# Weighting the norm and the split in the co-run with an attention's convolutions

## Chip, cores and metric

The kernel runs on one NeuronCore of a Trainium2 chip. The metric is the device time of one execution in microseconds. Three runs of the kernel before took 6441.66, 6464.38 and 6468.22 us; their median is 6464.38 us.

## What is computed

Two layers work on four images x of 96 channels and 128 x 128 pixels, in float32. The first is a state-space block with four scans over the pixels; the second is an attention made of convolutions. Cut to what matters here:

```
# layer 0, its end: LayerNorm over the 192 channels of ym, a 1x1 projection, the residual
yn = (ym - mean(ym, channel)) * rsqrt(var(ym, channel) + 1e-5) * ln_w + ln_b
x  = x + einsum('bdhw,cd->bchw', yn, out_w) + out_b
# layer 1, on group-normalised x
xr, x1, x2 = relu_split_norm(gn(x))        # positive part, negative part, each normalised over the whole image
key   = unfold(conv3x3(x1, aw1)); qry = unfold(conv3x3(x2, aw2))
attn  = softmax(key . qry / sqrt(C*9))     # one 96 x 96 x 9 kernel per image
y1    = layer_norm(conv3x3(conv3x3(x1, aw3), attn))
y2    = layer_norm(conv3x3(x2, w_conv2)) * x1
x     = x + xr + conv1x1(concat(y1, y2), w_full) + b_full
...
```

## The kernel before

The work is cut into generators. Each emits a few instructions, yields a cost (a number that the author chose, roughly microseconds), and goes on when it is asked again. Two of them are interleaved by `co_run(left, right, pace)` (L298): after each step of `left`, what it cost times `pace` is added to a debt, and `right` is advanced until the costs that it yields have paid the debt. So a smaller cost on the right means more of its steps beside one step on the left. Nothing else decides how densely two pieces of work lie beside each other; the order in which the built program issues then follows the emission closely, with small moves. [...]

The pieces that matter:

- **The norm**, `ssm_output` (L931), called by `Image.norm`: the end of layer 0 for one image, in 16 tiles of 1024 pixels and two more rounds for the pipeline's ends. A tile goes through loading y on SP's queue (L946), squares on ACT (L950), sums on PE (L960), a copy st (L972 or L974), four small transfers mq from st on ACT's queue (L979), a variance on DVE (L986 to L988), a root on ACT (L992), a reciprocal (L996), a write of rd to DRAM (L998) and a read back spread over 96 partitions as r (L1006), both on POOL's queue, the projection on PE (L1012), the product with r on DVE (L1025 or L1027), the residual on POOL (L1033 or L1035), statistics on DVE (L1039) and the store of xnew on SP's queue (L1088). The steps of one tile are spread over three rounds of six steps. The costs of an image sum to 149.6.
- **The split**, `split_norm` (L1091), called by `Image.split`: a first pass over 16 tiles (ACT L1137 and L1144, DVE L1140; cost 2.4 a tile), and a second pass (ACT L1253, DVE L1257) which also makes six planes of each half, for the x1 half on ACT and POOL (L1418 to L1432), for the x2 half on DVE (L1396 to L1410), at 6 x 2.5 a tile. It has almost no work on PE. The costs of image 1, 2 or 3 sum to 278.4.
- **The close**, `attn_output` (L2289), called by `Image.close`: the last 1x1 convolution and the residuals, 16 tiles, four DVE passes (L2274, L2279, L2280, L2316) and two sums (L2327 or L2329) a tile; cost 83.2 (166.4 for image 2).
- **The attention**, `attention` (L1949): 11 strips of 12 rows. In the map stage each strip runs `products` (L1446) four times: matmuls at L1467 and L1482, then evacuation by ACT (L1540) and DVE (L1554 to L1562). The transposes and products of the attention kernel (L1760, L1635) go between. A softmax follows (`weights`, with the transposes at L1701 in it), and the value stage, 11 strips with the kernel just made. The costs of an image sum to some 503. The attention also issues the loads of strips that lie two ahead (`ya`, L1903, copied to `yb` by ACT at L1928), and where these need the next image's planes, `until` (L2473) would force the split on.
- **The direct maps** of image 0, `direct_maps` (L2116): the same maps as plain 3x3 convolutions (matmuls at L2159), evacuated by ACT (L2177).

The order at the end of the program is: norm and split of image 0 beside the scan (L2546, pace 0.65); the direct maps of image 0 beside the scan and, when that is done, beside `light`, which is norm 1 and split 1 (L2560, pace 1.0); then for each image b its attention on the left, and on the right what is left of `light` and, chained behind it, norm b+1, split b+1 and the close of image b-1 (L2588 to L2608). Before images 2 and 3 what is left of `light` is drained without anything on the left.

Of the kernel before, what the change touches and what calls it, by code (L numbers as in the profile page):

```python
# [71 lines left out]
def kernel(  # L72
# [225 lines left out]
    def co_run(left, right, pace):  # L298


        owed = 0.0
        for cost in left:
            owed += cost * pace
            while owed > 0:
                got = next(right, 0)
                if got == 0:
                    return
                if got is None:
                    owed = 0.0
                    break  # L310
                owed -= got
# [39 lines left out]
    def chain(*gens):  # L351
        for g in gens:
            yield from g

    def drain(gen):
        for _ in gen:
            pass
# [68 lines left out]
    def project(b, weights, mv, beside, zb, xrows, ps):  # L426
# [10 lines left out]
        with tc.tile_pool(name="a2", bufs=2, side="left") as p2:  # L437
            each = len(beside)
            beside = chain(*(run(p2, 2, queue) for run, queue in beside))
            later, parts = Later(), {}  # L440
            y0s = []
# [1994 lines left out]
    class Image:  # L2436
# [50 lines left out]
    zb, yms = (  # L2487
        [dram.tile(shape, F32, name=f"{n}{p}", tag=f"{n}{p}", bufs=1) for p in range(npair)]
        for n, shape in (("zb", [2, 2 * C, NU, H, UW]), ("yms", [2, 2 * C, L]))
    )  # L2490
# [21 lines left out]
    with tc.tile_pool(name="wp", bufs=1, side="left") as wp:  # L2512
# [30 lines left out]
    imgs = {0: Image(0)}  # L2543
    imgs[0].begin()
    left = chain(imgs[0].norm(yms[0][0], psl, "left"), imgs[0].split(psl, "left"))
    co_run(left, last, 0.65)  # L2546
    drain(left)
# [5 lines left out]
    psr = ctx.enter_context(tc.tile_pool(name="psr", bufs=2, space=PSUM, side="right"))  # L2553
    imgs[1] = Image(1)
    imgs[0].lifting = True
    light = chain(
        imgs[1].norm(yms[0][1], psr, "right"),
        imgs[1].split(psr, "right", lambda i, second: second),
    )
    co_run(left, light, 1.0)  # L2560
# [22 lines left out]
    def maps_made(last):  # L2583
        maps_only.close()
        pool = ctx.enter_context(tc.tile_pool(name="e2", bufs=1, side="left"))
        last.kept = pool.tile([C, NS, SN], F32, name="e2")

    for b in range(NB):  # L2588
        after = []
        if b:  # L2590
            if b > 1:
                drain(light)
            imgs[b].begin()
            if b + 1 < NB:
                imgs[b + 1] = Image(b + 1)
                after.append(imgs[b + 1].norm(yms[(b + 1) // 2][(b + 1) % 2], psr, "right"))
                after.append(
                    imgs[b + 1].split(psr, "right", lambda i, second: second)
                )
            after.append(imgs[b - 1].close(psr, "right", 1.0 if b + 1 < NB else 2.0))  # L2600
            if b + 1 == NB:
                last = imgs[b].last = LastOutput(imgs[b], psr, "right")
                imgs[b].maps_made = lambda: maps_made(last)
                after += [last.before(), last.beside()]
        light = chain(light, *after)
        left = imgs[b].attend(at)
        co_run(left, light, 1.0 if b else 1.5)
        drain(left)  # L2608
# [79 lines left out]
```

## Time and profile before

| what | value |
|---|---|
| median of three runs | 6464.38 us |
| the profiled execution: time, span | 6470.83 us, 6468.9 us |
| busy share of the span: PE, DVE, ACT, POOL | 82%, 73%, 59%, 50% |
| mean granted clock of PE | 0.889 |
| busy share of the 16 DMA engines | 65.2% on q1, 2.2% on q0, 0.9% on q10 |

In the lines of the profile PE is TensorE, PEld its weight loads, DVE VectorE, ACT ScalarE, POOL GpSimd and SP the engine that issues most transfers. L1467 is a line of the kernel, printed as it was before the change. `out<-in` are names of tiles. A busy share is an average over stages with different limits, so it is the table of stages that has to be read; the prediction shows it. An fp32 matmul appears as two instructions, a transpose as one. After the scan ends near 3240 us, the stages follow one another in the order told above: the attention of image 1 begins near 3822 us, that of image 2 near 4700 us, that of image 3 near 5700 us, and the last output near 6428 us.

### The profile page before, as it was taken

What the parts mean: (1) busy time and instruction counts of PE and PEld (TensorE: products, weight loads), DVE (VectorE), ACT (ScalarE), POOL (GpSimd) and SP (SyncE); (2) the same over time, 40 slices, a digit from 0 to 9 for tenths busy, and PEclk for the clock granted to TensorE, in tenths of its full rate; (3) what the DMA queues carried; (4) which work ended last, traced back from release to release, by engine and by line L of the source; (5) the groups of instructions that cost most, each with busy time, mean ns of one, the idle gap of its engine ahead of it and who ended that gap; (6) DMA issues with size and microseconds to landing.
All of it is one profiled execution on the core that took longest, in us unless ns stands there. A gap on an engine that the chain in (4) does not pass through costs nothing. (4 is left out here: it accounts for less than half of the span.)

```text
span 6468.9 us, 76257 instructions
## 1 busy us (share of the span) xinstructions
PE 5321.3 (82%) x23264; PEld 2301.3 (36%) x23264; DVE 4711.2 (73%) x7132; ACT 3786.8 (59%) x4770; POOL 3238.6 (50%) x2472
## 2 busy tenths in 40 slices
PE   6889988987888753989988588877888877989888
PEld 2333323322222111444433234345333445345553
DVE  4247778988989668988934785468874587888757
ACT  1247767776787676777632565466533665545642
POOL 1226757978889544979821344346213266022310
PEclk9999989998998665999999799888988988999989
DMA  6767777775675766675666776665766655966668
GB/s 154 176 157 193 191 202 196 218 213 163 199 198 163 214 173 215 197 217 174 199 182 185 187 220 161 164 157 155 213 195 164 178 145 155 243 174 181 191 170 219
DMA packets 891433, 1205.18 MB, mean 186 GB/s; under 512 B 228533, under 2 KB 743483, under 8 KB 878545
## 3 DMA queue, kind: packets, MB, share of 16 engines
q1 hardware_dynamic: 860496, 1145.35, 65.2%
q0 software_dynamic: 16208, 38.41, 2.2%
q10 hardware_dynamic: 14320, 16.54, 0.9%
q8 instruction: 187, 3.06, 0.2%
q14 instruction: 222, 1.81, 0.1%
HBM read 777.82 MB, written 345.62 MB: 174 GB/s over the span
## 5 line engine op out<-in xcount | busy, mean ns | idle before, releaser
L629 PE MATMUL bank<-y,wp 128*128 128x512 f32 (+3 forms) x3584 | 1320.2, 626 | 84.5 <-DMA y<-y 40.9
L862 POOL TENSOR_TENSOR y<-y,dl 128x1024 f32<-128x1024 f32 x384 | 1062.5, 2767 | 273.1 <-DVE dl L854 247.9
L829 POOL TENSOR_TENSOR dl<-dl,u 128x1024 f32<-128x1024 f32 x384 | 1015.8, 2645 | 247.1 <-ACT dA L805 129.5
L850 DVE TENSOR_TENSOR_SCAN dA<-dA,pBC 128x512 f32<-128x512 f32 x768 | 981.6, 1278 | 30.7
L1467 PE MATMUL two<-ya,wd 128*64 128x192 f32 (+3 forms) x2376 | 590.6, 422 | 201.7 <-ACT odd L1540 77.1
L629 PEld LDWEIGHTS bank<-y,wp 128*128 128x128 f32 (+3 forms) x3584 | 459.3, 169 | 755.8 <-issue 658.0
L854 DVE TENSOR_TENSOR dl<-dA,pBC 128x512 f32<-128x512 f32 x768 | 528.4, 688 | 260.0 <-PE pBC L743 187.1
L2159 PE MATMUL bank<-y,wn 128*64 128x384 f32 (+5 forms) x2408 | 665.2, 501 | 52.7 <-DMA y<-x1d 28.3
L743 PE MATMUL pBC<-xr,wbc 60*128 60x512 bf16 (+1 forms) x1536 | 458.5, 405 | 301.3 <-DVE dA L850 230.9
L1928 ACT COPY yb<-ya 64x768 f32<-64x768 f32 (+1 forms) x660 | 537.5, 814 | 202.6 <-PE two L1467 128.7
L672 ACT ACTIVATE dl<-pd,dtb 128x512 f32<-128x512 f32 x768 | 486.3, 684 | 183.2 <-PE pd L743 166.8
L1467 PE MATMUL two<-yb,wd 128*64 128x192 f32 (+3 forms) x2376 | 566.4, 407 | 4.0 <-ACT yb L1928 4.0
L833 DVE TENSOR_TENSOR pBC<-dl,pBC 128x512 f32<-128x512 f32 x768 | 527.5, 687 | 8.1 <-POOL dl L829 7.1
L2159 PEld LDWEIGHTS bank<-y,wn 128*64 128x64 f32 (+3 forms) x2408 | 306.9, 167 | 340.2 <-issue 150.9
L805 ACT ACTIVATE dA<-dl,negA 128x1024 f32<-128x1024 f32 x384 | 420.3, 1142 | 2.3
L1467 PEld LDWEIGHTS two<-ya,wd 128*64 128x64 f32 (+1 forms) x2376 | 266.9, 169 | 399.5 <-ACT odd L1540 87.8
L672 ACT ACT_TABLE_LOAD x248 | 318.2, 1283 | 94.9 <-PE pd L743 81.6
L743 PEld LDWEIGHTS <-wbc 60*128 60x128 bf16 (+1 forms) x1536 | 102.9, 96 | 749.3 <-issue 736.1
L1467 PEld LDWEIGHTS two<-yb,wd 128*64 128x64 f32 (+1 forms) x2376 | 295.1, 170 | 153.6 <-issue 41.5
L1012 PE MATMUL bank<-y,outws 96*96 96x512 f32 x512 | 313.6, 752 | 11.4 <-DVE r L1025 8.7
L1467 PE MATMUL two<-ya,wa 128*96 128x384 f32 (+1 forms) x528 | 229.9, 519 | 72.1 <-DMA ya<-vp 27.4
L1540 ACT COPY odd<-two 128x384 f32<-128x384 f32 (+5 forms) x176 | 116.0, 659 | 286.7 <-PE two L1482 177.2
(316 smaller groups left out, 9210.2 us busy)
## 6 DMA issues: line engine op xcount, KB each, us to landing
u<-zb SPq DMA_DIRECT2D x192, 1024.0 KB
yms<-y SPq DMA_DIRECT2D x96, 512.0 KB
y<-yms SPq DMA_DIRECT2D x64, 768.0 KB
xn<-xnew SPq DMA_DIRECT2D x128, 384.0 KB
ya<-vp SPq DMA_DIRECT2D x120, 336.0 KB
y<-y SPq DMA_DIRECT2D x128, 258.2 KB
zb<-z SPq DMA_DIRECT2D x64, 512.0 KB
ya<-x1p SPq DMA_DIRECT2D x90, 336.0 KB
```

The source lines that it names most:

```text
L629: nc.tensor.matmul(blocks(pz[p:e]), lhsT=ws[k][:, d, c : c + e - p], rhs=window(ys[k], at, d, n), start=(i == 0), stop=(i == len(terms) - 1),)
L672: nc.scalar.activation(dst, src, AF.Softplus, bias=bias)
L743: nc.tensor.matmul(p, lhsT=w[rows], rhs=xr[rows, at : at + CH], start=True, stop=True)
L805: nc.scalar.activation(live[m]["dA"], live[m]["dl"], AF.Exp, scale=negA[:, g % 3, k : k + 1])
L829: nc.gpsimd.tensor_mul(t, t, u_view(n))
L833: nc.vector.tensor_mul(p, live[n]["dl"][:, bass.ts(half, CH)], p)
L850: nc.vector.tensor_tensor_scan(h, h, p, init, ALU.mult, ALU.add)
L854: nc.vector.tensor_mul(live[n]["dl"][:, sl], live[n]["dA"][:, sl], live[n]["C", half])
L862: nc.gpsimd.tensor_add(v, v, t.rearrange("p (a b) -> p a b", b=W))
L1467: nc.tensor.matmul(of(to[p:e], r), lhsT=w[:, i, c : c + e - p], rhs=tiles(t[k][PAIR[i]][:, SLOT[i]], o, r), start=(k == 0), stop=False,)
L1928: nc.scalar.copy(yb[k][64 * h - 64 : 64 * h, :, :n], ya[k][0:64, :, h * TN : h * TN + n])
L2159: nc.tensor.matmul(pc[p:e, :n].rearrange("p (h w) -> p h w", w=W), lhsT=w[:, c : c + e - p], rhs=v[:, :, 0:W], start=(i == 0), stop=(i == ...
```

## The change

A generator `weighed` passes on what another yields and scales each cost (a cost of `None` or 0 stays as it is). Norms 1 to 3 are weighed with 0.65, the splits of images 2 and 3 with 1.2. Split 1, the norm and split of image 0, the closes and everything else keep their costs. No instruction is added or removed; only where the pieces stand to each other is changed.

```diff
+    def weighed(gen, share):
+        for cost in gen:
+            yield cost and cost * share
...
     light = chain(
-        imgs[1].norm(yms[0][1], psr, "right"),
+        weighed(imgs[1].norm(yms[0][1], psr, "right"), 0.65),
         imgs[1].split(psr, "right", lambda i, second: second),
     )
     co_run(left, light, 1.0)
...
             if b + 1 < NB:
                 imgs[b + 1] = Image(b + 1)
-                after.append(imgs[b + 1].norm(yms[(b + 1) // 2][(b + 1) % 2], psr, "right"))
-                after.append(
-                    imgs[b + 1].split(psr, "right", lambda i, second: second)
-                )
+                norm = imgs[b + 1].norm(yms[(b + 1) // 2][(b + 1) % 2], psr, "right")
+                split = imgs[b + 1].split(psr, "right", lambda i, second: second)
+                after += [weighed(norm, 0.65), weighed(split, 1.2)]
             after.append(imgs[b - 1].close(psr, "right", 1.0 if b + 1 < NB else 2.0))
```

## The prediction

> **What bounds the kernel now.** I read the page first: PE is busy 82% of the span, DVE 73%, and the chain that ended last covers only the last 1%, so no single chain bounds the run and the answer lies in stages. I therefore took the busy time of each engine in each stage that the change touches. Columns: from:to and length, then busy time (and instructions) of PE, weight loads, DVE, ACT, POOL, granted clock, DMA share, GB/s.
>
> ```profile
> core 0: us, PE busy (x) PEld busy (x) DVE busy (x) ACT busy (x) POOL busy (x), PEclk, DMA share, GB/s
> 2107.00:2375.00 268.00, 192.65 (x498) 45.92 (x497) 177.94 (x247) 170.61 (x188) 145.75 (x103) 0.67 0.72 208
> 3245.00:3535.00 290.00, 249.48 (x906) 97.13 (x901) 117.13 (x253) 84.97 (x125) 66.10 (x64) 0.91 0.69 185
> 3535.00:3640.00 105.00, 65.19 (x281) 38.72 (x280) 72.08 (x159) 62.86 (x112) 20.50 (x24) 0.85 0.66 176
> 3822.00:3957.00 135.00, 113.72 (x735) 66.31 (x736) 103.20 (x190) 71.96 (x99) 68.86 (x103) 0.89 0.66 171
> 3957.00:4245.00 288.00, 248.18 (x1298) 111.30 (x1296) 120.76 (x265) 128.69 (x171) 101.31 (x132) 0.88 0.60 159
> 4245.00:4525.00 280.00, 216.88 (x1474) 140.51 (x1474) 225.73 (x454) 185.20 (x276) 147.74 (x212) 0.84 0.61 158
> 4525.00:4690.00 165.00, 140.48 (x515) 62.11 (x516) 137.19 (x249) 99.93 (x129) 51.49 (x75) 0.91 0.78 213
> 4690.00:4815.00 125.00, 99.53 (x287) 37.70 (x286) 106.46 (x125) 45.12 (x44) 12.73 (x13) 0.85 0.71 203
> 4815.00:5100.00 285.00, 245.64 (x1258) 107.88 (x1255) 123.35 (x274) 124.02 (x165) 103.42 (x136) 0.87 0.64 168
> 5100.00:5470.00 370.00, 289.69 (x2021) 185.40 (x2021) 297.07 (x584) 241.63 (x351) 201.69 (x291) 0.86 0.61 160
> ```
>
> The rows are, in order: the norm of image 0 beside the scan; the norm of image 1 beside image 0's direct maps, and what follows it; attention of image 1 (the rest of split 1, norm 2, split 2, then the value stage with the rest of split 2, then a lump, the close of image 0); norm 3 and split 3. The reader is to see three things. Every norm takes 285 to 290 us, whatever stands beside it, and 268 us even beside the scan, where no engine is busy over 72%. Beside a norm PE is busy 86% and DVE 43%; beside a split both are near 80%. And in the lump PE has little to do.
>
> Next, what ends the waits of a norm stage (4815 to 5100), for DVE, and one place in it for PE:
>
> ```profile
> DVE mq L986 <- DMA mq<-st: 56.9, 12, 10.0
> DVE xstats L1039 <- POOL r L1033: 28.3, 25, 2.4
> DVE r L1025 <- DMA r<-rd: 23.8, 6, 8.3
> ```
>
> ```profile
> 4963.99 1.28 DVE L1025 TENSOR_TENSOR r<-bank,r 96x512 f32<-96x512 f32 x2 [9.35 <-issue]
> ...
> 4968.08 0.32 ACT L992 ACTIVATE mq<-mq,eps 32x32 f32<-32x32 f32 x1 [5.16 <-DVE mq L988]
> ...
> 4969.14 1.65 PE L1467 MATMUL two<-ya,wd 128*128 128x384 f32 x2 [6.44 <-ACT kt L1765]
> ...
> 4970.71 1.06 PE L960 MATMUL bank<-y,mean 96*32 96x512 f32 x1
> ```
>
> DVE waits for the norm's own transfers (mq from st, then r from rd), in order: r's, issued at 4955.27 in this view, is what the 9.35 us go to. ACT waits behind DVE for the root; a convolution's copy kt stands behind that root, and PE idles 6.4 us. So a norm tile (285 us over 16 tiles, some 17 us) is set partly by a chain with three DMAs in it (the table of issues gives 4.1 us to landing for rd and 4.2 for r), not by PE's work alone.
>
> **A page that bears on it.** The Trainium skill, "TensorE: Matmul & The Clock Gate", Part 1 on the HAM clock gate, says that PE's clock falls to half after an idle window of some 3.4 us. The last two rows agree: behind 6.4 us of idling a matmul of L960 takes 1.06 us, against 0.59 us in the same view before it. The forecast goes by the stage rows, which hold this already; but it warns that a norm stage with less work on PE may idle more and run slower per matmul. For the transfers, "DMA: Bandwidth & Descriptors", Latency and other measured facts, gives about 2 us of fixed cost; the trace has 4.1 and 4.2, and I use the trace.
>
> **The change part by part.** It adds no instruction, transfer or wait; it changes how much of the convolutions is emitted between two steps of the norm and the split. The costs that a norm reports are multiplied by 0.65 (149.6 becomes 97), a split's of images 2 and 3 by 1.2 (278.4 becomes 334), so more or fewer steps fit into the same convolutions. I counted, in the order in which the two built programs issue on each engine, the convolution matmuls that stand in each stretch:
>
> ```
> stretch on PE                              before  after
> inside norm 1 (direct maps)                   259    161
> end of norm 1 to end of direct maps           174    272
> end of direct maps to norm 2                  609    333
> inside norm 2                                 451    311
> norm 2 to the softmax of image 1              881   1297
> inside norm 3                                 455    310
> norm 3 to the softmax of image 2             1165   1320
> ```
>
> The other queues go along: SP issues the loads of y and the stores of xnew between fewer ya loads of the convolutions, ACT the mq transfers between fewer yb copies, POOL the rd and r transfers behind fewer plane sums. Nothing else moves; image 3's attention has neither norm nor split beside it. No split has to be forced before the loads of the next image in either version.
>
> Prices. (1) A norm with 31 to 38% fewer convolutions. Norm 3 loses 145 matmuls (254 of 1258 instructions). Upper bound: the stage shrinks as its instructions do, 20% of 285 = 57 us. Lower bound: it is held by its chain, as norm 0 was at 268 us, so 17 us. I take the middle, 35 us for each of the three norms.
>
> (2) What is taken from the norms comes back elsewhere. The 98 direct-map matmuls (178 instructions) at PE's 65.19/281 = 0.232 us are +41 us; at that stretch's whole length, 105/174 = 0.60 us a matmul, +59. Image 1: 35 off for the norm, 41 on: **+6** (bounds -16 and +42).
>
> (3) Attention of image 1 up to its softmax. Split 1 is further along by then, so 276 matmuls before norm 2 go: 276 x 0.318 (135 us by the 424 matmuls that 735 instructions make at split 3's 2021/1165) = -88. Norm 2: -35. Split 2: +416 matmuls, together with 14 more of its 64 steps (62 of 64 instead of 48 stand ahead of the softmax). DVE: of 226 us, about 97 are evacuation (881 x 0.11, from that engine's groups between 5170 and 5470), 129 split; after, 129 x 62/48 + 1297 x 0.11 = 310 us. PE: 217 x 1297/881 = 319 us. At the 80% which split 3 reached, PE gives 400 us against 280, so about +122 (bounds +114, +132). Sum **-1** (bounds -31 and +27).
>
> (4) Value stage of image 1 and the lump, 165 + 125 = 290 us, DVE busy 244 (84%). The order shows 2 of 16 tiles of the close of image 0 ahead of the value stage's end before, and 11 after; 2 of split 2's steps are left instead of 16. That takes some 30 us of DVE work (of 48 us of split groups there) out of a stretch that DVE fills, and the closing tiles find convolutions beside them: 214/0.84 = 254, a gain of 36. As the value stage with a close beside it is no better packed elsewhere, I take **-30** (bounds -15, -45).
>
> (5) Attention of image 2: norm -35; split 3 +155 matmuls: PE 290 x 1320/1165 = 329, at 80% 411 us, +41; DVE 297 + 155 x 0.11 = 314, at 80% 393, +23. I take +35: **0** (bounds -34, +32).
>
> Sum: 6 - 1 - 30 + 0 = -25 us on the profiled execution's own 6470.8: 6446. That execution lies 6.4 us above the median of the three runs, 6464.4, so **6440** in their terms. The cover: the moved matmuls are nearly all paid again beside the splits; what is really saved is the lump.
>
> **Rivals.** *The norm gives way fully* (each norm -57, the rest as above): its 86% of PE busy speaks for it, the 268 us of norm 0 against. 3 x 22 us more: about 6375. *The norm holds its pace* (slower): the three-DMA chain sets a tile's time, each norm gives back only 17 us, and the moved matmuls pay the full stage rate beside the split (+59, +132, +49 with 155 x 0.318), the tail giving -15. Its parts are then +42, +27, -15 and +32, +86 in sum, 6550 as the median; with the forecast's own prices for the moved matmuls (+41, +122, +35) and tail it is +29, 6494. I put it at 6520. It decides when a tile stays above about 16 us with 310 matmuls beside the norm; 285 to 290 us for three norms with different work beside them, and 268 for the fourth, speak for it; that POOL had 2.7 us scan operations ahead of norm 0's transfers speaks against. *The tail gives nothing*: the close is only spread under a value stage which DVE fills already (137 of 165 us), so the 30 us come back: 6470. That the change would not do what it says is excluded by the order: the counts above moved.
>
> **How the numbers follow.** Forecast 0.50, norm gives way 0.15, norm holds 0.22, tail gives nothing 0.13. Half a percent, 32 us, is about what a measurement of this kernel can tell from no change: faster is below 6432, slower above 6497. The forecast's own range is 6405 to 6475, and 0.23 of its 0.50 lies below 6432. Faster 0.15 + 0.23 = 0.38; same 0.27 + 0.13 = 0.40; slower 0.22. The range runs from 6385 to 6525: it reaches towards both outer cases and leaves out about a tenth at each end.
>
> **What would show it.** In the changed profile a norm of image 2 or 3 should last 240 to 260 us (under 235: gives way; over 265: holds); norm 3 to the softmax of image 2 should last 395 to 415 us with PE and DVE near 80%; the stretch from the softmax of image 1 to norm 3 should fall from 290 to about 260 us, and the closing tiles of image 0 should lie mostly inside the value stage. The forecast is wrong if PE's idle per norm tile grows while the tile keeps its length, or if the split stage takes the 155 matmuls for nothing.

## The result, and the profile after

The changed kernel takes 6501.01 us (median of 6 runs, 6486.87 to 6512.99), the kernel before 6462.57 (median of 6 in the same comparison). The ratio is 1.0064, 95% interval 1.0053 to 1.0076: **slower by 0.64%, 38 us** by the medians (the expectations below write 39). The profiled execution after took 6503.85 us with a span of 6501.8, against 6468.9 before, so the two traces differ by 33 us, and it is these 33 us that the stages below account for.

All the stages of the table are cut at the same events in both traces: a norm from its first square on ACT to the start of its last statistics on DVE, a softmax at its first transpose. The last columns give the convolution matmuls that stand in the stretch, counted in the order in which PE's instructions are issued; they include the transposes and products of the attention kernel.

| stretch | before us | after us | difference | forecast | matmuls before | after |
|---|---|---|---|---|---|---|
| norm 1 | 281.8 | 250.4 | -31 | -35 | 259 | 161 |
| end of norm 1 to softmax of image 0 | 120.6 | 192.2 | **+72** | +41 | 174 | 272 |
| softmax of image 0 to norm 2 | 306.2 | 227.1 | -79 | -88 | 609 | 333 |
| norm 2 | 281.9 | 267.4 | -15 | -35 | 451 | 311 |
| norm 2 to softmax of image 1 | 289.0 | 407.1 | +118 | +122 | 881 | 1297 |
| softmax of image 1 to norm 3 (value stage, lump) | 291.8 | 257.5 | -34 | -30 | 333 | 323 |
| norm 3 | 274.1 | 228.0 | -46 | -35 | 455 | 310 |
| norm 3 to softmax of image 2 | 383.0 | 434.5 | **+52** | +35 | 1165 | 1320 |
| the rest (start to norm 1, and behind) | 4240.4 | 4237.5 | -3 | 0 | | |

Time by stage of the kernel after, in the columns of the prediction's table. The rows are norm 1 and what follows it, norm 2, its split, value stage and lump, norm 3, its split:

```profile
3243.00:3493.00 250.00, 206.59 (x712) 77.92 (x713) 93.95 (x205) 77.37 (x109) 64.85 (x64) 0.84 0.68 181
3493.00:3675.00 182.00, 122.28 (x475) 66.80 (x473) 133.65 (x256) 92.43 (x158) 59.15 (x68) 0.82 0.66 176
3913.00:4180.00 267.00, 223.68 (x1021) 88.35 (x1019) 105.05 (x220) 107.92 (x142) 87.89 (x108) 0.82 0.57 151
4180.00:4587.00 407.00, 321.49 (x2218) 205.52 (x2218) 315.39 (x616) 258.86 (x374) 216.35 (x316) 0.85 0.60 155
4587.00:4845.00 258.00, 222.13 (x800) 96.99 (x801) 212.59 (x330) 124.85 (x148) 27.59 (x50) 0.92 0.79 213
4845.00:5073.00 228.00, 210.22 (x968) 83.75 (x968) 101.01 (x218) 103.69 (x137) 87.22 (x106) 0.88 0.68 179
5073.00:5508.00 435.00, 332.33 (x2325) 212.95 (x2326) 341.41 (x653) 266.60 (x386) 231.02 (x336) 0.87 0.59 153
```

Read it from the top. In the second row PE is busy 122 of 182 us, 67%, hardly more than the 62% of the prediction's row for this stretch, although the moved matmuls now stand there: they wait. In the two split rows PE and DVE are busy 76 to 79% each, as the forecast's "80%" had it, and the stretch grew all the same. The value stage and lump fell as forecast, with PE up from 83 to 86%.

What DVE waits for in norm 3 of the kernel after (engine, what it was about to run, what it waited for: us in total, times, longest):

```profile
DVE mq L990 <- DMA mq<-st: 38.8, 10, 7.0
DVE xstats L1043 <- POOL r L1037: 32.0, 24, 4.9
DVE r L1029 <- DMA r<-rd: 22.6, 7, 7.0
```

The order is the one of before, the first of the three is down from 56.9 us: DVE still waits for the norm's own transfers. That they set the norm's length is not shown by this: PE is busy 210 of the 228 us of norm 3 now, 92%, against 86% before.

### The profile page after: what moved, and what is told of

Same layout as the page of the kernel before. It is cut to its first block, busy times and chain, and to the rows that moved or that the text cites. A ratio compares the mean times of both kernels' runs of the same rounds, so it can differ in the third digit from the quotient of the medians.

```text
span 6501.8 us, 76298 instructions
## 1 busy us (share of the span) xinstructions
PE 5339.0 (82%) x23264; PEld 2310.7 (36%) x23264; DVE 4732.1 (73%) x7132; ACT 3786.5 (58%) x4770; POOL 3242.5 (50%) x2472
## 5 line engine op out<-in xcount | busy, mean ns | idle before, releaser
L2163 PE MATMUL bank<-y,wn 128*128 128x384 f32 (+5 forms) x2408 | 681.6, 509 | 83.7 <-DMA y<-x2d 38.6
L2163 PEld LDWEIGHTS bank<-y,wn 128*128 128x128 f32 (+3 forms) x2408 | 314.1, 170 | 374.1 <-issue 182.4
L1016 PE MATMUL bank<-y,outws 96*96 96x512 f32 x512 | 333.6, 795 | 11.7 <-DVE r L1029 10.0
```

The source lines that it names most:

```text
L2163: nc.tensor.matmul(pc[p:e, :n].rearrange("p (h w) -> p h w", w=W), lhsT=w[:, c : c + e - p], rhs=v[:, :, 0:W], start=(i == 0), stop=(i == ...
```

## The experiments

Theory S (after the result): what norm 1 gives is taken back at a higher price where the matmuls land, since the direct maps' loads stand behind late transfers in SP's queue. Its rivals are told where they were tested. A price here is the difference of a stretch between two kernels over the difference of convolution matmuls in it. Stretches are from one execution each and single executions of one kernel differ by some 10 us, so a price from one stretch is known to about 0.1 us; ratios are from several runs. Norm 2 varied more: with 0.65 it lasted 240 us with 291 matmuls in one kernel below, and 267 with 311 in the kernel after.

### Which of the weights does it: norm 1 alone, the later ones alone

```diff
-                after += [weighed(norm, 0.65), weighed(split, 1.2)]
+                after += [norm, split]
```

> Only norm 1 is weighed (0.65); norms 2, 3 and splits 2, 3 keep their costs. Theory S (the 98 matmuls moved out of norm 1 land where the direct maps' loads stand behind late plane stores in SP's queue, so they come back dearer than they were): from the start of norm 1 to the softmax of image 0 some 440 us as in the changed kernel (411 before), the close of image 0 still goes beside the value stage (about -34), matmuls ahead of norm 2 come back beside split 2; sum about 0, 6465 (6450 to 6480). Rival N (the loss lies in the later norms and splits, this part is as cheap as forecast): 6435.

Measured 6458.49 us, ratio 0.9997 (0.9987 to 1.0006). Norm 1 lost 31 us, the stretch behind it gained 73, and the stretch to norm 2 gave 80 back, 306 to 226. The sum came out as theory S had it and theory N fell; SP's queue itself is put to the test further down. The second run keeps only the later weights (norm 1's `weighed` removed):

> Norm 1 keeps its cost; norms 2 and 3 are weighed with 0.65, splits 2 and 3 with 1.2. Theory S: the stretch up to the softmax of image 0 is that of before (411 us); the lump at the close of image 0 stays (split 1 is no further along), attention of image 1 pays +15 to +25, of image 2 about +6: 6470 to 6495. Rival N: the loss of the change is all here and the gain of the lump is missing: above 6500. If the direct maps were all of it and the later parts were neutral: 6463.

6495.51 us, 1.0051 (1.0031 to 1.0071). Norm 2 lost 42 us for 160 matmuls, the stretch behind it gained 47; norm 3 lost 39 for 190, the stretch behind it gained 57 for 144; the value stage and the lump stayed at 295. The total is just above the upper edge of theory S (6470 to 6495). So the lump gives its 34 us only when split 2 has been brought forward: by norm 1's weight in the changed kernel, and in a run below by lighter norms 2 and 3 with the splits at their own costs. Most of the loss comes with the later weights.

### Norms or splits: the two later weights apart

```diff
-                after += [weighed(norm, 0.65), weighed(split, 1.2)]
+                after += [norm, weighed(split, 1.2)]
```

and, for the second, `after += [weighed(norm, 0.65), split]`, both without the weight on norm 1.

> The kernel before with splits 2 and 3 weighed with 1.2 and the norms at their own costs. The matmuls ahead of either softmax stay (881 and 1165), only fewer of the split's steps stand beside them. Theory C (beside a split the convolutions run at their own pace of 0.33 us a matmul, and the split is hidden whatever its density): norm 2 to the softmax of image 1 289 us and norm 3 to that of image 2 383 us as before, within 10; what is left of the splits goes into the value stages, so 6475 to 6500. Rival P (the split's steps set the stretch): 250 and 340 us, and as much back later.

> The kernel before with norms 2 and 3 weighed with 0.65 and nothing else: 160 and 155 matmuls go from the norms to the stretches behind them. Theory C: norms about 40 us less each (240, 232), the stretches behind them +53 and +51 (342, 434) at 0.33 us a matmul, the close of image 0 goes beside the value stage (-30): 6440 to 6460. Rival P (the split sets its stretch, more matmuls go in for nothing): stretches 300 and 395, 6380.

Splits only: 6503.14 us, 1.0063 (1.0041 to 1.0085), a little beyond the expected 6475 to 6500. With the same matmuls behind each norm and fewer split steps beside them, the stretches took 284 us (289 before) and 363.5 (383), while the steps that were not made there lengthened the next two stretches by 39 and 40 us. Norms only: 6472.41 us (20 runs), 1.0013 (1.0002 to 1.0023): norms -30 and -36, the stretches behind them +69 for 160 matmuls and +60 for 155, the tail -31. So **the 1.2 alone costs as much as the whole change**: thinning the split speeds the convolutions beside it by 5 and 20 us, and its left-over steps stand later, where the stretches grow by 39 and 40 (norm 3, with fewer matmuls, gave 18 back). In the changed kernel these two costs can't be added up: beside light norms the 1.2 costs less, 23 us (6495.51 against 6472.41). Theory C held in the main, with one stretch 20 us shorter and the norms-only kernel somewhat dearer than expected.

### The opposite weights

```diff
+                after += [weighed(norm, 1.35), weighed(split, 0.82)]
```

> The opposite change on the kernel before: norms 2 and 3 weighed with 1.35 and splits 2 and 3 with 0.82 (673 and 659 convolution matmuls inside the norms instead of 451 and 455). Theory L (in a norm a matmul costs 0.28 us, the slope from 455 to 310 matmuls; beside a split 0.37): norm 3 lasts about 331 us, norm 3 to the softmax of image 2 about 315, gain 10 to 15 us for each of two images, 6440. Rival O (the costs before were near the best and both slopes bend): norms over 345 us or the split stretch above 335 us, 6465 to 6500.

6462.62 us (12 runs), 0.9999 (0.9985 to 1.0014). Norms 2 and 3 took 31 and 33 us more for 222 and 204 more matmuls, 0.14 and 0.16 us each; the stretches behind them lost 59 and 46 us for 222 and 192 fewer, 0.27 and 0.24 each. Adding convolutions to a norm is cheaper than what the same convolutions cost beside a split; the close and value stages gave it back (+8 and +23 us). Neither expectation was met in full: the norms were shorter than theory L had them (norm 3 307 us, not 331), the stretch behind norm 3 longer (336, not 315). In these norms PE's busy time rose by 34 and 46 us, as much as their length or more, so the low price is not evidence that transfers hold them.

### What the convolutions cost with less split beside them

The splits of images 2 and 3 are weighed with 20, so that less of them lies beside the map stages and the rest is made uncovered later; the second kernel adds 0.65 for norms 2 and 3.

```diff
+                after += [norm, weighed(split, 20.0)]
...
+                after += [weighed(norm, 0.65), weighed(split, 20.0)]
```

> The kernel before with the costs of splits 2 and 3 times 20, so that nearly nothing of them lies beside the convolutions behind norms 2 and 3 (they are made up, uncovered, before the next image's attention; the whole run gets longer for that and isn't the point). In the trace of the kernel before, the last map stage (image 3, nothing but the close beside it, and from 6150 us nothing) runs at 100 us for some 665 PE instructions, 0.15 us each or 0.26 us a convolution matmul. Theory F (the convolutions have a pace of their own, and that is the floor of the price): the 881 matmuls from norm 2 to the softmax take 225 to 245 us (289 before), the 1165 behind norm 3 take 300 to 320 us (383 before). Theory G (the stretch is held by something else, such as the loads of strips, and the split lies in its gaps): both stay above 270 and 360 us.

> The same with norms 2 and 3 times 0.65: 1041 instead of 881 matmuls behind norm 2, 1300 instead of 1165 behind norm 3, with nearly no split beside them. Theory F: the two stretches are longer than those of the run beside it by 0.26 us a matmul, +42 us for 160 and +35 us for 135, so that the moved matmuls' price of 0.4 us (+69 for 160, +60 for 155 in the run with the light later norms) is 0.26 us of the convolutions' own and the rest the split's. Theory G: +64 and +54 us, at 0.4 us each, without the split as with it.

6550.77 and 6559.00 us, ratios 1.0138 (1.0109 to 1.0168) and 1.0151 (1.0103 to 1.0199); the uncovered splits are in these. The stretches behind norms 2 and 3 took 251 and 325 us, a little over theory F's band, and 160 and 135 matmuls more cost +37 us each, 0.23 and 0.28 us, near theory F's 0.26. But the split had not gone as far as was expected: its first pass is still there whole, and of the second pass 17 of 48 instructions (L1257 of the kernel before, L1261 here) behind norm 2 and 28 of 64 behind norm 3. These are prices beside a thinner split, not beside none. The stretch behind norm 3 with the thinner split, then with more matmuls, in the two kernels:

```profile
5133.00:5458.00 325.00, 266.92 (x2014) 174.16 (x2014) 218.68 (x465) 206.19 (x302) 130.57 (x211) 0.92 0.57 146
```

```profile
5091.00:5453.00 362.00, 305.68 (x2289) 199.46 (x2290) 236.87 (x509) 226.19 (x329) 145.05 (x237) 0.91 0.57 145
```

PE is at 82 to 84% here, DVE at 65 to 67%. The larger part of the split that the kernel before has in this stretch fills DVE to 80% and makes it only 58 us longer (383 against 325). That **the convolutions have a pace of their own** is seen without a split in the trace of the kernel before, in the last map stage, beside the close and then, from 6158 us, beside nothing of the kind:

```profile
6000.00:6100.00 100.00, 89.41 (x661) 56.50 (x650) 80.84 (x125) 65.70 (x82) 37.56 (x50) 0.98 0.72 201
6150.00:6250.00 100.00, 84.72 (x667) 58.32 (x665) 53.28 (x112) 49.51 (x70) 27.16 (x55) 0.88 0.60 150
```

Both hundred microseconds hold about 665 PE instructions, with DVE at 81% or at 53%: 0.15 us an instruction, and at 1.75 instructions a convolution matmul (2038 for 1165 behind norm 3) 0.26 us.

### The dear stretch behind norm 1: SP's queue

In the kernel after, what PE waited for in this stretch, then what SP stood at before issuing (3493 to 3675 us):

```profile
PE bank L2163 <- DMA y<-x2d: 33.7, 4, 16.7
PE bank L2163 <- DMA y<-x1d: 9.3, 1, 9.3
PE bank L2163 <- ACT value L2181: 5.2, 2, 3.6
```

```profile
SPq L1444 <- DVE plv L1400: 19.4, 4, 9.5
SPq L1105 <- DVE xn L1144: 18.4, 10, 5.0
SPq L1444 <- DVE c2a L1796: 13.7, 2, 11.5
SPq L1105 <- DVE half L1261: 9.8, 2, 8.6
```

PE lacks y, the input of the direct maps, 43 us in all. In the kernel before, in the 121 us of this stretch, it was one wait:

```profile
PE bank L2159 <- DMA y<-x1d: 14.0, 1, 14.0
```

SP issues y's loads, but stands at stores of planes (L1444) and loads of split 1 (L1105) whose data or buffers DVE has yet to deliver. One place in that order, SP's timeline (start, length, line, transfer):

```profile
3621.69 0.56 SPq L1444 DMA_DIRECT2D x2p<-plv  x1
3633.26 0.55 SPq L1444 DMA_DIRECT2D vp<-plv  x1
3633.91 4.89 SPq L2146 DMA_DIRECT2D y<-x2d  x7
```

SP stands 11 us at the store of vp, planes of the lifts that the direct maps make beside the split; behind it y. The matmul that needed that y, in PE's timeline of the same window:

```profile
3638.58 6.65 PE L2163 MATMUL bank<-y,wn 128*128 128x384 f32 x13 [9.26 <-DMA y<-x2d]
```

The stores of split 1's planes and of the lifts were given to POOL's queue, on the kernel after and on the kernel before:

```diff
-                        store_planes(nc.sync, m, i * RS, RS, pl)
+                        store_planes(
+                            nc.gpsimd if keep is imgs[1].keep else nc.sync, m, i * RS, RS, pl
+                        )
...
-                        lambda pl, a=a: store_planes(nc.sync, img.vp, a, LR, pl), LR, vector=True,
+                        lambda pl, a=a: store_planes(nc.gpsimd, img.vp, a, LR, pl), LR, vector=True,
```

> The changed kernel, but the plane stores of split 1 and of the lifts in the direct maps are issued by POOL instead of SP, so that the direct maps' loads on SP's queue don't stand behind them. Theory S: PE's wait for y<-x2d and y<-x1d in the stretch after norm 1 (43 us) mostly goes, softmax of image 0 comes 25 to 35 us earlier, 6470. Rival W (the 98 matmuls simply cost that much there: PE, ACT and DVE work, not the queue): within 10 us of 6501.

> The same edit on the kernel before, as a control. Theory S: the stretch after norm 1 has 14 us of PE waiting for y there, so at most 10 to 15 us less: 6450 to 6463. Rival W: the same as before within 10 us. A slowdown would say that POOL's waiting for the planes costs more than SP's.

On the kernel after 6495.52 us, 1.0049 (1.0033 to 1.0065), within the 10 us of rival W: the stretch fell only from 192 to 186. SP now stood at the xn loads of the split, 40 us, as its waits show:

```profile
SPq L1105 <- DVE xn L1144: 22.1, 12, 5.0
SPq L1105 <- DVE half L1263: 18.0, 4, 7.2
```

On the kernel before it gained 29 us unasked: 6433.16 us, 0.9958 (0.9943 to 0.9973); both expectations missed it. The stretch from the softmax of image 0 to norm 2 fell from 306 to 274 us. But the built order moved as well, and this move was not small: on PE norm 2 now begins earlier among the convolutions, and holds some 578 convolution matmuls instead of 451 (counted in the two traces). So the gain can come from SP's queue or from the other order; the runs don't part the two. With this edit on both the change costs 62 us instead of 38. Then all splits' stores, on both (theory Q: stores on SP are what holds the split stages):

```diff
-                        store_planes(nc.sync, m, i * RS, RS, pl)
+                        store_planes(nc.gpsimd, m, i * RS, RS, pl)
```

> The kernel before, with the plane stores of all splits and of the lifts issued by POOL instead of SP. The run with those of split 1 alone gained 29 us, all of it (32 us) where the rest of split 1 stands beside the attention of image 0 and 1 (stretch from the softmax of image 0 to norm 2). Theory Q (beside an attention, the strip loads ya stand behind plane stores in SP's queue, in every split): splits 2 and 3 gain too, 20 to 40 us each, 6370 to 6410. Rival: it was particular to split 1 beside a value stage: 6433.

> The changed kernel with the same edit. Theory Q: a good part of the dear price of a convolution matmul beside a split (57 us for 155 matmuls, 0.37 each, in the runs so far) was SP's queue, so without it the change is worth 20 us more than it was: after minus before, with both edited, is 0 to +20 instead of +39. Rival D (DVE and the other engines set the price): the difference stays +30 to +45.

6425.65 us, 0.9943 (0.9923 to 0.9963), and 6511.85 us, 1.0081 (1.0060 to 1.0102). The change costs 86 us on this ground instead of 38; in the kernel before, the stretches to norms 2 and 3 gain 35 and 28 us, those behind norms 2 and 3 lose 19 and 31. Theory Q fell, and the difference is beyond its rival's band too. Last, the first edit with split 1's xn loads on POOL's queue too:

```diff
-                    nc.sync.dma_start(y, xnew[:, bass.ts(t, SN)])
+                    eng = nc.gpsimd if 1 in imgs and keep is imgs[1].keep else nc.sync
+                    eng.dma_start(y, xnew[:, bass.ts(t, SN)])
```

> The changed kernel with the plane stores of split 1 and of the lifts, and the loads xn of split 1, issued by POOL. With the stores alone moved, SP still stood 40 us in the direct-map stretch at loads xn that wait for DVE to free their buffer, and PE still waited 27 us for y. Theory S (any wait of split 1 in SP's queue holds the direct maps' loads up): the stretch from the end of norm 1 to the softmax of image 0 falls from 186 us to 150 to 165, 6470 in all. Rival W (engine work sets the stretch): stays at 180 to 195.

> The kernel before with the edit of e7 (plane stores of split 1 and of the lifts, and split 1's loads xn, by POOL): the fair partner of e7, which ran at 6445. Theory S: there was little to win in the direct-map stretch (121 us), the gain is that of e4 (the rest of split 1 beside the attention of images 0 and 1), 6425 to 6435; so with SP's queue relieved the change costs some 10 to 20 us instead of 39. Rival: 6406 or less, the change costs 39 us with or without the edit.

On the kernel after 6445.23 us (20 runs), 0.9977 (0.9966 to 0.9989); on the kernel before 6429.43, 0.9949 (0.9932 to 0.9966). The kernel after gained more than expected (6470), and the stretch behind norm 1 fell to 169 us, 4 above theory S's band and below rival W's. PE's waits for y there are nearly gone:

```profile
PE bank L1708 <- DVE sm L1699: 15.9, 1, 15.9
PE bank L1642 <- ACT kt L1631: 15.7, 5, 5.0
PE bank L2166 <- ACT value L2184: 8.7, 4, 5.8
PE bank L2166 <- DMA y<-x1d: 3.4, 1, 3.4
...
PE bank L2166 <- DMA y<-x2d: 1.0, 1, 1.0
```

From 43 us to 4.4, with the same matmuls in norm 1 and in the stretch. In the kernel before the same edit brings the stretch from 121 to 113 us, so the 98 matmuls cost 55 us now, 0.56 each instead of 0.73: SP's queue made 17 of the 72 us. Of the 55, PE's busy time is 48 (120 against 72 us in the two stretches), more than the 41 forecast; the rest was not taken further. In all the change costs 16 us on this ground instead of 38, but that is not this stretch alone: here too norm 2 of the kernel before holds some 578 matmuls instead of 451, so that the weights move others than they did.

The Trainium skill, "DMA: Bandwidth & Descriptors", Issuing engines are not separate DMA queues, says that issuing from several engines saves only the time of initiating transfers, usually small. Here the transfers stayed as they were, and 39 us of PE's waits for y went with another issuing engine (43 to 4.4): what was saved was no time of initiating, but a load's wait behind transfers that stood waiting for their producers. In such a case the measurement decides.

### The split's PSUM bank

In the stretch behind norm 3 of the kernel before, ACT waits 34 us for the bank into which it writes the split's scaled pieces. Theory A: that bank sets the price beside the split. The edit writes the pieces into the split's own SBUF tile, on the kernel before and on the kernel after:

```diff
-                        f = part(ps, C, k, TN) if planes else o
+                        f = o
```

> The kernel before; the splits of images 1 to 3 write their scaled pieces on ACT straight into half (SBUF) instead of into a PSUM bank, and DVE works on them in place. Theory A (beside a split ACT stands behind L1253, which waits for DVE to free one of two banks, 34 us between norm 3 and the softmax of image 2, and the convolutions' copies odd, ends and kt stand behind it): that stretch falls from 383 us to 350 to 365, 6400 to 6430 in all. Rival B (ACT then waits for half itself, which POOL and DVE free later, or the convolutions' pace has another cause): 375 us or more, 6455 or more.

> The changed kernel with the same edit. Theory A: the stretch from norm 3 to the softmax of image 2 falls from 434 us to 390 to 410, and the change, after minus before with both edited, costs 20 us or less instead of 39. Rival B: 425 us or more, the change costs 30 to 45 us as it did.

6549.03 us, 1.0122 (1.0105 to 1.0140), and 6519.61 us, 1.0079 (1.0060 to 1.0097). ACT's wait did not go, it moved. ACT's waits behind norm 3, before and then with this edit:

```profile
ACT bank L1253 <- DVE half L1257: 34.1, 16, 6.5
```

```profile
ACT half L1253 <- DVE diff L1408: 22.5, 9, 9.7
ACT half L1253 <- POOL pl L1429: 17.3, 5, 4.7
```

40 us instead of 34, and the stretch went from 383 to 406 us, as rival B had it. As the wait was not removed, theory A isn't refuted; a separate tile with more buffers wasn't tried. With both edited, the change is a gain of 29 us, where rival B expected a cost of 30 to 45. It is no proof of theory A, whose stretch got longer with the edit, 442 us instead of 434; the gain stays unexplained.

### A better version

From the prices: norm 1 light (it brings split 2 forward and evens out the lump), norms 2 and 3 heavier, splits denser, and SP relieved as above.

```diff
-                after += [weighed(norm, 0.65), weighed(split, 1.2)]
+                after += [weighed(norm, 1.2), weighed(split, 0.88)]
```

> e7 with norms 2 and 3 weighed with 1.2 and splits 2 and 3 with 0.88: norm 1 light (its matmuls no longer stand behind split 1's waits in SP's queue, and the close of image 0 still goes beside the value stage), the later norms heavy. Theory L (a matmul costs 0.16 to 0.28 us inside a norm and 0.33 beside a split): norm 3 about 292 us, norm 3 to the softmax of image 2 about 355, 6410 in all. Rival: gains as little as e9 did, 6440.

6412.37 us (4 runs, 6397.91 to 6418.24), 0.9917 (0.9900 to 0.9934): ahead of both kernels, 52 us below the kernel before in the same comparison (6464.59). Of this the edit of the queues alone gives 35 on the kernel before (6429.43); the weights bring some 17 more. Norm 3 came out at 293 us as expected, the stretch behind it at 375 instead of 355. Norm 2, its split, norm 3, its split:

```profile
3878.00:4165.00 287.00, 266.83 (x1623) 127.15 (x1620) 143.31 (x326) 147.62 (x199) 111.52 (x152) 0.98 0.69 181
4165.00:4490.00 325.00, 242.76 (x1712) 158.71 (x1710) 268.52 (x518) 217.87 (x319) 186.21 (x265) 0.85 0.62 160
4750.00:5045.00 295.00, 268.93 (x1434) 122.51 (x1433) 129.41 (x289) 136.03 (x181) 108.72 (x146) 0.90 0.65 172
5045.00:5420.00 375.00, 281.73 (x1856) 181.39 (x1855) 299.62 (x573) 233.53 (x341) 203.31 (x286) 0.82 0.57 150
```

Norm 2 holds 669 convolution matmuls and takes 285 us from event to event; with 451 it took 282, with 311 it took 267. It is the cheapest case: with the opposite weights it held 673 and took 313.

## Why the prediction was wrong

The forecast was 6440, a small gain that the scatter might hide; it came out at 6501, a loss clear of the scatter. The direction was wrong because what was taken from the norms came back dearer than it was priced: step 2 and step 5 failed, and norm 2 gave less than it should. By its steps:

1. **Norms, -35 each: nearly right in sum, by luck.** They gave 31, 15 and 46, 92 instead of 105. By the prediction's own signs norm 2 (267 us) holds and norm 3 (228) gives way; neither lies in its 240 to 260. Matmuls taken out brought 0.10 to 0.32 us each, matmuls put in cost 0.14 and 0.16 (opposite weights). That a chain of transfers sets the norm's pace is not shown: in norm 3 after PE is busy 92%. Two of its figures were off as well. Cut at events, the norms last 282, 282 and 274 us and norm 0 254, not 285 to 290 and 268, which were rounded windows. And r's 4.2 us is the landing of 384 KB (the table of issues), so of the two transfers only rd's 4.1 us for 4 KB stands beside a fixed cost.
2. **The return behind norm 1, +41: failed,** and with +72 went beyond its upper bound of +59. The price was PE's busy time, 0.232 us an instruction, or at most the stretch's own rate. But the 98 matmuls need y, and y's loads stand on SP's queue behind stores and loads that wait for DVE; PE waited 43 us for y where it had been 14. Shown: with these taken off SP's queue the return is +55, so the queue made 17 of the 31 us that were missing. Half of the rest is PE's busy time, 48 us where 41 were forecast; the other half is open. The prediction had said that SP issues the loads "between fewer ya loads"; who waits behind whom on SP it didn't ask.
3. **Attention of image 1 to its softmax:** -79 and +118 against -88 and +122, right in size; norm 2 gave 20 less. This step priced its matmuls at 122/416 = 0.29 us (its own figures give 119 to 120, a slip that changes nothing).
4. **Value stage and lump, -30: right,** -34. DVE's busy time there fell from 244 to 213 us, as it was argued. That PE has little to do in the lump was misread: the prediction's row has it busy 99.53 of 125 us, 80%.
5. **The return behind norm 3, +35: failed in size,** +52, above its upper bound of +49. 35/155 is 0.23 us a matmul, below the 0.26 which the same convolutions take in the last map stage with nothing beside them. Shown: beside a thinner split they cost 0.23 and 0.28; beside the split 0.28 to 0.43 in the kernels where matmuls were added. Busy time over 80% was read as if the engines' sums were what sets the stretch, but the lower bound (DVE's sum, +23) is no bound when the convolutions alone need more.

The differences add up to the error in the traces' terms: 13 us from the norms, 31 from step 2, 9 and -4 from step 3, -4 from step 4, 17 from step 5, -3 from the rest, 59 in all; the forecast of -25 becomes +33 with the rounding. The time is near the rival "norm holds its pace", but not by its mechanism: in sum the norms gave nearly what was forecast, not 17 us each, and the return was dearer.

On the clock the prediction's warning, drawn from the Trainium skill, "TensorE: Matmul & The Clock Gate", Part 1 (the clock goes by how busy PE has been of late), came true in part: norms 1 and 2 with fewer matmuls ran at a granted clock of 0.84 and 0.82 (0.91 and 0.88 before), norm 3 kept its 0.87. That this is why norm 2 gave only 15 us is argued, not shown. It fits that in the kernel after with SP relieved the same norm with some 30 matmuls more ran at 0.91 and took 248 us, PE busy 206 us instead of 224.

**Open:** what of the price beside splits 2 and 3 lies above the convolutions' 0.26 us, since ACT's wait for the split could only be moved; the rest of the 0.56 us behind norm 1; what sets the length of a norm; and why the edits of the queues make the kernel before faster, since they also moved the built order.

## What to carry to other kernels

Before giving work out anew between stages, find for each stage the price of one unit more of it: here the norm, where DVE is busy some 40%, took more for little (0.14 to 0.16 us a matmul), and the stretch beside a split, where PE and DVE are both near 80%, returned it at its full pace or dearer (0.28 to 0.43). The least price is the pace of that work where nothing stands beside it, which the trace often shows somewhere. And follow each moved instruction to the queue that feeds it: a load that stands behind a store waiting for another engine adds to the price, whatever PE's busy time says (17 of 72 us here). Count the order again after such an edit: here it moved more than the edit seemed to say.

## What the runs showed of the hardware that had not been expected

- With the plane stores of split 1 and of the lifts issued by POOL instead of SP the kernel before was 29 us faster (0.9958), and with those of all splits 0.9943, though POOL's queue also carries the norm's rd and r transfers. The built order changed with it, so the queue is not shown to be the cause.
- Norm 2 with 669 matmuls beside it had the granted clock at 0.98 and took 285 us, with 311 it had 0.82 and took 267. It is no rule: with 673 it had 0.92 and took 313, and with some 343 it had 0.91 and took 248.
- Writing the split's pieces into an SBUF tile rather than a PSUM bank made the kernel before 1.2% slower (1.0122): ACT then waited 40 us behind norm 3 for that tile instead of 34 for the bank.
